# A narrower weight load and a changed order in the nine products of a scan step

## The chip, the cores and the metric

The kernel runs on one core of one Trainium2 chip. The metric is the device time of one launch in microseconds (us). Three runs of the kernel before are shown. A profile is one further execution, recorded by the hardware profiler.

## The reference

The input is a batch of 32 images of 48 channels, 64 rows and 128 columns in float32. Two layers follow each other. Each normalizes its input over groups of three channels, sends it through four scans and adds the result to its own input. Cut to what matters:

```python
def _conv1d(x, w, b):                       # 5 taps, 48 to 48 channels
    y = jax.lax.conv_general_dilated(x, w, window_strides=(1,), padding=[(2, 2)],
                                     dimension_numbers=('NCH', 'OIH', 'NCH'))
    return y + b[None, :, None]
def step(w, b):
    def f(carry, inp):
        nxt = inp + _conv1d(carry, w, b)
        return (nxt, nxt)
    return f
# rows downward (down_w), rows upward (down_w again), columns to the right (right_w),
# columns to the left (left_w): each is lax.scan(step(w, b), first, rest)
x = x + _L0_conv_ref(_gn(x), ...)
x = x + _L1_conv_ref(_gn(x), ...)
```

A step of a scan can't begin before the step ahead of it has ended: each takes the whole result of the last row (or column), convolves it along the row (or column) and adds the next input. There are 63 steps down, 63 up, 127 to the right and 127 to the left.

## The kernel before

**A step as nine products.** A row has 128 positions. Eight neighbouring positions and 48 channels make 384 pairs (position e from 0 to 7, channel), which are spread over three tiles of 128 partitions, called thirds here. The table `PIECES` says which position lies where: third 0 holds the positions 0 and 1 whole and 32 channels of position 2; third 1 holds 16 channels of position 2, then positions 3 and 4, and 16 channels of position 5 in its partitions 112 to 127; third 2 holds positions 6 and 7 and the rest of 5. Along the free dimension lie the 16 blocks of eight positions and 8 images, so 128 elements (for a column scan: 8 blocks of 8 and, again, the images and the halves of a pair of image groups, 128 elements too).

The convolution is then a product of a banded 384 x 384 matrix with the row. `PRODUCTS` lists its nine non-zero blocks as (input third i, output third o, shift s): seven within the block of eight and two across its border, (0, 2, 1) and (2, 0, -1), which read the neighbouring block. The border products have 96 weight columns (`BORDER`) and leave out the block at the edge, so that they stream 120 elements in a row step and 112 in a column step. All others have 128 weight columns (`FULL`) and stream 128. Five taps reach two positions far, so a part of a block can be zero: the weights are laid into zeroed tiles.

`step` walks through `PRODUCTS` in its order and issues one float32 matmul each (L706) into one of three PSUM tiles, one for each output third. The first product of an output third starts its accumulation, the last one ends it, and after it VectorE adds the bias and the input and writes the new row (L715). In the order of before, output third 0 is complete after five products, output third 2 after six and output third 1 after all nine. The next step begins with products of the input thirds 0 and 2; the first that needs third 1 is (1, 0, 0), its fifth. In the trace each float32 matmul stands as two weight loads (LDWEIGHTS) and two matmuls.

**The phases.** `PHASES` is an order of twelve phases written out by hand: eight row phases (down and up, for each of four groups of eight images in each of two layers) and four column phases (right and left, for each of two pairs of groups in each layer). Tiles are named after layer, group or pair and way: `step_01u` is layer 0, group 1, upward, `step_11l` layer 1, pair 1, to the left. A row phase has 126 steps, a column phase 254, and all together 2024.

**The work around the steps.** Everything else is put into the program between two steps by an agenda of due times, counted in steps: loading and storing rows and columns (SP's queue, some on ACT's and POOL's), scaling of the input by the normalization (ACT, L579), the additions of the residual (POOL, L638), permutations (POOL and ACT, L536 and L663), and the statistics, which use a few small matmuls of TensorE (L298 and L302). `in_order` keeps each engine in the order of the program. Each transfer or operation waits by semaphores for what it needs.

Of the kernel before, what the change touches and what calls it, by code (L numbers as in the profile page):

```python
# [33 lines left out]
C = 48  # L34
# [9 lines left out]
FULL = 128  # L44
# [22 lines left out]
    (2, 0, -1),  # L67
    (1, 0, 0),
    (1, 2, 0),
    (0, 1, 0),  # L70
    (1, 1, 0),
    (2, 1, 0),
)
BORDER = 2 * C


def weight_runs():
# [41 lines left out]
def kernel(  # L119
# [573 lines left out]
    def step(key, weights, b_at, src, inp, dst, whole, part):  # L693


        ps = [
            ps_step.tile([FULL, N], F32, tag=f"step{o}", name=f"step{o}_{key}")
            for o in range(NG)
        ]
        left = [sum(1 for p in PRODUCTS if p[1] == o) for o in range(NG)]  # L700
        seen = [0] * NG
        for i, o, s in PRODUCTS:
            seen[o] += 1
            m = BORDER if s else FULL
            at = FULL * (o - NG * s - i + 1)
            nc.tensor.matmul(  # L706
                part(whole(ps[o])[0:m], -s),
                weights[:, i, at : at + m],
                part(src(i), s),
                start=seen[o] == 1,  # L710
                stop=seen[o] == left[o],
            )
            if seen[o] == left[o]:
                layer, way = b_at
                nc.vector.scalar_tensor_tensor(  # L715
                    dst(o),
                    whole(ps[o]),
                    bd[:, o, layer, way : way + 1],
                    inp(o),
                    ALU.add,  # L720
                    ALU.add,
                )

    def row_step(k, h, prev, inp, name):
        _, layer, g = PHASES[k]

        def part(t, s):
            return t[:, max(0, s) * GB : N + min(0, s) * GB]

        step(  # L730
            f"{layer}{g}{name}{h}",
            wt[f"down{layer}"],
            (layer, DOWN),
            lambda i: prev[:, i],
            lambda o: inp[:, o],
            lambda o: row(k, h)[:, o],
            lambda ps: ps,
            part,
        )

    def col_step(k, way, v0, v1):
        _, layer, pair = PHASES[k]

        def col(v):
            kb, e = divmod(v, E8)
            j, kk = divmod(kb, KQ)
            view = slot[slots(k)[j % 3]].rearrange(
                "p (o m e k b) -> p o e k m b", o=NG, e=E8, k=KQ, b=GB
            )
            return lambda o: view[:, o, e, kk]  # L750

        def part(t, s):
            t = t.rearrange("p (s a) b -> p s a b", s=2)
            return t[:, :, max(0, s) : NH + min(0, s)] if s else t

        step(
            f"{layer}{pair}{'drl'[way]}{v1}",
            wt["right" if way == RIGHT else "left"],
            (layer, way),
            col(v0),  # L760
            col(v1),
            col(v1),
            lambda ps: ps.rearrange("p (m b) -> p m b", b=GB),
            part,
        )
# [422 lines left out]
```

## Time and profile before

| | |
|---|---|
| median of three runs | 4323.13 us (4319.51, 4324.4, 4323.13) |
| time of the profiled execution | 4327.19 us |
| its span, from the first to the last instruction | 4325.4 us |
| mean granted TensorE clock in the span | 0.979 |
| first matmul of a step, last matmul of a step (from the span's start) | 109 us, 4241 us |
| TensorE matmul busy | 4072.9 us (94%) |
| TensorE weight load busy | 4042.5 us (93%) |
| VectorE busy | 2177.4 us (50%) |
| ScalarE busy | 1337.2 us (31%) |
| GpSimd busy | 891.9 us (21%) |

Busy is the union of the durations of an engine's instructions. PE stands for TensorE's matmuls, PEld for its weight loads, which run beside the matmuls, DVE for VectorE, ACT for ScalarE, POOL for GpSimd and SP for SyncE, which issues transfers only. A line of a group names the source line, the engine, the operation, the tiles (out<-in), the active rows and weight columns of TensorE (128*96), partitions and elements streamed (128x112) and the count; then, behind the bar, busy time in us, the mean ns of one record, and behind the next bar the idle time just before these records with what ended most of it. A line of windows gives the stretch in us, its length, the busy time of the five engines, the granted clock, the share of the DMA engines' time and GB/s.

### The profile page before, as it was taken

How to read it: one execution, taken by the hardware profiler on the slowest of the kernel's cores; microseconds unless marked ns; L12 is line 12 of the kernel's file. 1: busy time of each engine (PE TensorE's matmuls, PEld its weight loads, DVE VectorE, ACT ScalarE, POOL GpSimd, SP SyncE). 2: the span in 40 equal slices, each digit the busy share in tenths (PEclk: the TensorE clock that was granted, in tenths of full speed). 3: DMA queues.
4: the chain of work that ended last, by engine and by line, in shares of the span. 5: the costliest groups of instructions: out<-in, count | busy, mean ns of one | idle time of the engine just before them, and what ended most of it. 6: DMA issues, size and time to landing. Idle time of an engine off the chain costs nothing. (4 is left out here: it accounts for less than half of the span.)

```text
span 4325.4 us, 89999 instructions
## 1 busy us (share of the span) xinstructions
PE 4072.9 (94%) x36624; PEld 4042.5 (93%) x36624; DVE 2177.4 (50%) x6554; ACT 1337.2 (31%) x2656; POOL 891.9 (21%) x859
## 2 busy tenths in 40 slices
PE   3898998998999999998999999999999999999992
PEld 1898998998999999998999999999999999999992
DVE  6344444446764445444446655444444444444443
ACT  1683301344794554300005773513000002110122
POOL 3472001234323010000004310000000024510352
PEclk9999999999999999999999999999999999999996
DMA  9999799966998989769507989929289049999999
GB/s 165 183 188 166 111 157 158 235 130 191 237 204 138 158 152 159 117 115 174 131 1 218 220 173 144 153 45 160 47 136 202 1 77 242 249 241 158 176 197 183
DMA packets 2117983, 680.35 MB, mean 157 GB/s; under 512 B 2006688, under 2 KB 2057408, under 8 KB 2077632
## 3 DMA queue, kind: packets, MB, share of 16 engines
q1 hardware_dynamic: 2019552, 582.30, 71.9%
q10 hardware_dynamic: 94816, 86.00, 9.7%
q0 software_dynamic: 3200, 6.30, 0.6%
q8 instruction: 288, 4.72, 0.5%
q14 instruction: 127, 1.04, 0.1%
HBM read 397.57 MB, written 295.99 MB: 160 GB/s over the span
## 5 line engine op out<-in xcount | busy, mean ns | idle before, releaser
L579 ACT ACTIVATE arena<-arena,offset,scale 128x256 f32<-128x256 f32 (+2 forms) x816 | 576.4, 800 | 423.9 <-PE step_12u L706 120.5
L638 POOL TENSOR_TENSOR arena<-arena 128x2048 f32<-128x2048 f32 x80 | 362.8, 4548 | 1469.2 <-PE step_10l L706 459.0
L536 POOL COPY arena<-arena 112x256 f32<-112x256 f32 x458 | 271.2, 651 | 561.5 <-DMA arena<-in_x 282.6
L706 PE MATMUL step_00r<-arena,early 128*128 128x128 f32 x2286 | 252.4, 274 | 15.3 <-DMA arena<-upa 14.2
L706 PEld LDWEIGHTS step_00r<-arena,early 128*128 128x128 f32 x2286 | 251.9, 187 | 15.8 <-issue 15.8
L706 PE MATMUL step_01r<-arena,early 128*128 128x128 f32 x2286 | 251.6, 274 | 14.0 <-DMA arena<-upa 14.0
L706 PEld LDWEIGHTS step_01r<-arena,early 128*128 128x128 f32 x2286 | 251.4, 187 | 14.2 <-issue 14.1
L706 PE MATMUL step_11r<-arena,early 128*128 128x128 f32 x2286 | 252.1, 274 | 8.6 <-DVE arena L715 8.6
L706 PEld LDWEIGHTS step_11r<-arena,early 128*128 128x128 f32 x2286 | 251.6, 187 | 9.0 <-DVE arena L715 8.9
L470 ACT ACTIVATE early<-arena 128x256 f32<-128x256 f32 x192 | 129.6, 675 | 412.2 <-DMA arena<-xin 319.9
L706 PE MATMUL step_00l<-arena,wleft 128*128 128x128 f32 x2286 | 252.2, 274 | 0.0
L706 PEld LDWEIGHTS step_00l<-arena,wleft 128*128 128x128 f32 x2286 | 251.8, 187 | 0.0
L706 PE MATMUL step_10l<-arena,wleft 128*128 128x128 f32 x2286 | 249.1, 272 | 0.0
L706 PE MATMUL step_11l<-arena,wleft 128*128 128x128 f32 x2286 | 249.1, 272 | 0.0
L706 PE MATMUL step_01l<-arena,wleft 128*128 128x128 f32 x2286 | 249.1, 272 | 0.0
L706 PE MATMUL step_10r<-arena,early 128*128 128x128 f32 x2286 | 249.1, 272 | 0.0
L706 PEld LDWEIGHTS step_10l<-arena,wleft 128*128 128x128 f32 x2286 | 249.0, 186 | 0.0
L706 PEld LDWEIGHTS step_11l<-arena,wleft 128*128 128x128 f32 x2286 | 249.0, 186 | 0.0
L706 PEld LDWEIGHTS step_01l<-arena,wleft 128*128 128x128 f32 x2286 | 249.0, 186 | 0.0
L706 PEld LDWEIGHTS step_10r<-arena,early 128*128 128x128 f32 x2286 | 249.0, 186 | 0.0
L663 ACT COPY arena<-arena 128x256 f32<-128x256 f32 x172 | 99.6, 656 | 404.2 <-POOL arena L638 152.9
L403 ACT ACTIVATE early<-arena 112x512 f32<-112x512 f32 x192 | 121.1, 631 | 305.6 <-DMA arena<-in_x 237.7
(176 smaller groups left out, 7070.1 us busy)
## 6 DMA issues: line engine op xcount, KB each, us to landing
arena<-in_x SPq DMA_DIRECT2D x48, 768.0 KB, 12.7
xin<-arena SPq DMA_DIRECT2D x96, 384.0 KB, 5.6
arena<-xin SPq DMA_DIRECT2D x96, 384.0 KB, 8.9
mid<-arena SPq DMA_DIRECT2D x96, 384.0 KB, 7.9
arena<-mid SPq DMA_DIRECT2D x192, 192.0 KB, 4.3
upb<-arena SPq DMA_DIRECT2D x192, 192.0 KB, 3.9
arena<-upb SPq DMA_DIRECT2D x96, 384.0 KB, 12.7
arena<-xin SPq DMA_DIRECT2D x186, 192.0 KB, 4.2
```

Source lines behind the costliest of these rows:

```text
L403: nc.scalar.activation(junk[0:P], piece, AF.Identity, accum_out=self.sum[:, at[0], at[1]],)
L470: nc.scalar.activation(junk[:, 0:n], view[:, b], AF.Identity, accum_out=self.sum[:, i, j : j + 1])
L536: copy(dst[:, r, q], src[:, r0 + r, q])
L579: nc.scalar.activation(args[0], args[0], AF.Identity, bias=args[2], scale=args[1])
L638: eng.tensor_tensor(unit, unit, nat, ALU.add)
L663: copy(by_w(perm)[:, a], src[:, a])
L706: nc.tensor.matmul(part(whole(ps[o])[0:m], -s), weights[:, i, at : at + m], part(src(i), s), start=seen[o] == 1, stop=seen[o] == left[o],)
```

## The change

The order of `PRODUCTS` changes in its last three entries: the product of input third 1 with output third 1 now comes before that of input third 0 with output third 1. The number of weight columns comes from a table, `COLUMNS`. The two border products keep their 96, and (0, 1, 0) has 128 - 48/3 = 112 instead of 128. It leaves out the partitions 112 to 127 of output third 1, which belong to position 5; the input third 0 holds positions 0 to 2, more than two away, so that these weights are zero. As (0, 1, 0) no longer writes all partitions, it can't be the product that starts the accumulation, which (1, 1, 0) does now. It streams 128 elements as before.

```diff
@@ -67,11 +67,12 @@
     (2, 0, -1),
     (1, 0, 0),
     (1, 2, 0),
+    (1, 1, 0),
     (0, 1, 0),
-    (1, 1, 0),
     (2, 1, 0),
 )
 BORDER = 2 * C
+COLUMNS = {(0, 2, 1): BORDER, (2, 0, -1): BORDER, (0, 1, 0): FULL - C // 3}
@@ -701,7 +702,7 @@
         for i, o, s in PRODUCTS:
             seen[o] += 1
-            m = BORDER if s else FULL
+            m = COLUMNS.get((i, o, s), FULL)
             at = FULL * (o - NG * s - i + 1)
```

## The prediction

> **What bounds the kernel now.** I read the page's engine table first, then TensorE's groups with the shapes kept apart, then the windows, and last the places where TensorE waits.
>
> ```profile
> span 4325.4 us, 89999 instructions
> PE 4072.9 (94%) x36624; PEld 4042.5 (93%) x36624; DVE 2177.4 (50%) x6554; ACT 1337.2 (31%) x2656; POOL 891.9 (21%) x859
> ```
>
> TensorE is the bound outside the head, the tail and some gaps; DVE has half its time free. The page's chain view helps with nothing here: it ends in one ScalarE copy of the last outputs.
>
> ```profile
> L715 DVE SCALAR_TENSOR_TENSOR arena<-step_10l,bd,arena 128x128 f32<-128x128 f32 x381 | 122.0, 348 | 126.9 <-PE step_10l L706 126.9
> L715 DVE SCALAR_TENSOR_TENSOR arena<-step_13u,bd,arena 128x128 f32<-128x128 f32 x186 | 59.5, 347 | 63.2 <-PE step_13u L706 63.0
> 3233.00:3482.00 249.00, 249.00 (x2289) 249.00 (x2288) 122.30 (x382) 0.00 (x0) 0.00 (x0) 1.00 0.46 97
> ```
>
> A step ends with three DVE additions, so busy plus idle over the steps is the step's period: (122.0 + 126.9)/127 = 1.960 us for a column step, (59.5 + 63.2)/62 = 1.979 for a row step. The window shows TensorE without a gap at full clock. There are 8 x 126 row and 4 x 254 column steps, 2024 in all.
>
> A step has 9 matmuls, each standing as two weight loads and two matmuls: 18 slots. What a slot costs comes out of the groups, because busy is a union: in a burst of k back-to-back records it is (k - 1) slots plus one record.
>
> ```profile
> L706 PE MATMUL step_10l<-arena,wleft 128*96 128x112 f32 x508 | 69.4, 259 | 0.0
> L706 PE MATMUL step_13u<-arena,early 128*96 128x120 f32 x252 | 36.1, 266 | 0.0
> L302 PEld LDWEIGHTS ps_r<-mean_c_r,maskp 112*128 112x128 f32 x24 | 3.0, 192 | 0.0
> L298 PEld LDWEIGHTS ps_r<-dev_r,mask_in 128*112 128x112 f32 x24 | 2.7, 178 | 0.0
> ```
>
> The border products (96 weight columns) come in fours, once per step. With 112 streamed columns: (69.4/127 - 0.259)/3 = 95.8 ns a slot; with 120: (36.1/63 - 0.266)/3 = 102.3 ns. The weights are the same, only the stream differs: these slots are **bound by the stream**, 0.82 ns a column, and 128 columns extrapolate to 109 ns. The two statistics rows stream only 8 columns, in bursts of six, so they show the **weight load**: 128 columns (3.0/4 - 0.192)/5 = 111.6 ns, 112 columns (2.7/4 - 0.178)/5 = 99.4, and 98.3 between the starts of single records (the rounding of 2.7 allows 97 to 102). So a slot is the longer of its weight load and the stream before it. A step adds up: 14 loads of 128 columns at 111.67 + one stream of 128 (into the first border product) 109.17 + 3 x 102.5 = 1980 ns; for columns 3 x 95.83 gives 1960. Both agree with the periods, which confirms 109.17.
>
> **What the Trainium skill says.** "TensorE: Matmul & The Clock Gate", section "LDWEIGHTS (loading the stationary operand)": a load takes its columns divided by 1.2, so 128 cost 106.7 and 112 cost 93.3 ns; the trace agrees on the difference (111.6 - 98.3 = 13.3) and adds 5 ns to each. The same page, "Back-to-back issue gap": N/2.4 + 2.5 ns for one pass. "FP8 and Floating Point Precision", "TensorE Precision Notes": true FP32 takes four passes. Two passes a record make 2 x 8/2.4 = 6.7 ns per 8 columns, as the border rows show. "Perfetto Trace Analysis", "Tensor Engine Instruction (MATMUL, LD_WEIGHTS)": a record starts with the prefetch and its end is estimated, so I use intervals, not durations.
>
> **The change part by part.**
>
> *The narrow load.* In each step the two loads of the third's product (0,1,0) shrink from 128 to 112 columns, 13.3 ns each. The stream beside them keeps 128 columns: the slot falls from 111.67 only to 109.17, by **2.5 ns**. 2 x 2.5 = 5.0 ns a step: 1.975 us for rows, 1.955 for columns. Times 2024: **10.1 us**. From both ends: 0, if the stream of 128 costs as much as its load; 13.3 ns a slot, 54 us, if loads could run ahead. I take 2.5, because in the border bursts loads of 96 columns keep strictly to the stream's 95.8 or 102.3 ns and gain nothing by being shorter.
>
> *The exchange.* (1,1,0) now opens the accumulation of output third 1 and (0,1,0) follows. Both inputs were waited for earlier in the step (third 0 at its first product, third 1 at (1,0,0)), and the DVE addition that frees third 1's accumulator is the one that (1,0,0) waits for. No wait, DMA or queue entry is added; SP, ACT and POOL keep their order. The last product is still (2,1,0), at the same place before the next step's four leading products, so the about 0.2 us between the end of DVE's third addition and the load that waits for it stays. Cost: 0; if that cover were gone, a DVE addition (0.35 us) would stand bare in each step.
>
> *The border products* take their 96 columns from a table instead of a condition: the same instructions, 0.
>
> *What swallows part of it.* The gain reaches the end only where the next gap follows TensorE's pace.
>
> ```profile
> L706 PE MATMUL step_00d<-arena,early 128*128 128x128 f32 x882 | 115.7, 283 | 23.7 <-DVE arena L715 16.9 <-DVE arena L590 6.8
> L706 PE MATMUL step_01d<-arena,early 128*128 128x128 f32 x882 | 112.3, 279 | 15.9 <-DVE arena L715 15.9
> L706 PE MATMUL step_02u<-arena,early 128*128 128x128 f32 x882 | 111.7, 278 | 9.3 <-DVE arena L715 9.3
> L706 PE MATMUL step_01r<-arena,early 128*128 128x128 f32 x1778 | 223.4, 278 | 14.0 <-DMA arena<-upa 14.0
> L706 PE MATMUL step_11r<-arena,early 128*128 128x128 f32 x1778 | 223.6, 277 | 8.6 <-DVE arena L715 8.6
> 4241.00:4326.00 85.00, 0.15 (x2) 0.00 (x0) 24.68 (x19) 18.89 (x33) 20.50 (x22) 0.51 1.28 174
> ```
>
> Each gap returns the gain made since the event that started the chain it waits for. The gaps of 00d and 01d (to 435 us) wait for input that arrives at its own pace; 141 steps lie before them: -0.7. The gap at 1363 (02u) hangs on input statistics whose chain TensorE last released at 1239: 62 steps, -0.3. The 14 us before 00r and 01r are a write and read back of the last rows, about 20 steps each: -0.2. Some 6 us in 11d around 2535 to 2572 follow a release at 2472: -0.3. The 8.6 us of 11r (at 3857) wait for loads behind a spill that starts with the step at 3794: 32 steps, -0.2. In the tail DMA is full (share 1.28), but its engines stood idle at 4053 to 4062 until TensorE released the results; only what is gained after that can vanish, 95 steps: -0.4. At half clock, some 11 steps: -0.1. Together -2.2.
>
> **Sum.** 10.1 - 2.2 = 7.9 us, 0.18%. The profiled execution took 4327.2 us around its span of 4325.4 and would come to 4319.3; the median of the runs shown is 4.1 us lower, 4323.1, and comes to **4315.2 us**. 0.2%, about what a measurement of this kernel can tell from no change, is 8.6 us: the forecast lies close under it.
>
> **The rivals.**
>
> *Nothing happens (chance 0.11).* The stream of 128 costs 111.67 itself, or the gaps swallow all. For it: recorded starts into the first border product lie 112 apart, although that load has 96 columns. Against it: then the step would be 2.5 ns longer than its period unless the way back into wide loads were shorter. Time: 4322 to 4324.
>
> *Loads run ahead (0.06).* Both loads give 13.3 ns: 26.7 a step, 54 us, 4269; half of it 4296. For it: the page above lets a weight load overlap earlier matmuls. Against it: the lockstep of the border bursts.
>
> *The switch back to wide loads costs (0.11), the slower end.* After a border burst the interval behind the first wide matmul is recorded as 118 ns in rows and 125 in columns, 6.5 and 13.3 over the usual. If that is a real restart cost, the change adds one more switch a step, at (2,1,0): 1008 x 6.5 + 1016 x 13.3 = 20 us, less 10 gained: +10, 4333. It decides from 5 ns a switch, where the gain is used up; from 9.3 the kernel is slower by over 0.2%. Against it: the interval ahead of it is short by as much (102.5 and 95.8), and 118.2 - 111.67 and 125 - 111.67 are just 109.17 less the two border streams: the start is recorded early, when the short stream ends, while the load is still running. With a 128-column stream this should vanish.
>
> **How the numbers follow.** My own case has 0.72. Its range is 4311 to 4319: from no loss in the gaps (10.1) and 2 us of run scatter below, to a loss of 4 and some scatter above; the runs shown differ by 4.9 us. Of it 0.30 gains over 8.6 us and 0.42 less. Faster by over 0.2%: 0.30 + 0.06 = 0.36. Within: 0.42 + 0.11 = 0.53. Slower: 0.11. The range of 8 in 10 takes in the case without effect and leaves out the far ends: 4310 to 4324.5.
>
> **What would show it.** In the profile after, the L715 groups give 1.975 and 1.955 us a step; the group 128*112 with 128 streamed columns appears in 4048 records; weight loads of 112 columns stand 109 ns apart. 1.98 and 1.96 would mean the stream costs what the load did, 1.953 and 1.933 that loads run ahead, over 1.98 a switch cost. If the periods are right and the time is not, the gaps at 1363, 2535, 3857 or the tail have grown by more than the 2.2 us above.

## The result and the profile after

| | before | after |
|---|---|---|
| median of 22 runs | 4324.85 us (4316.24 to 4334.18) | 4317.7 us (4301.99 to 4326.45) |
| profiled execution: time, span | 4327.19, 4325.4 us | 4318.23, 4316.5 us |
| ratio of the times | | 0.9982, interval 0.9974 to 0.9990 |

The changed kernel is faster by 0.18% (0.10 to 0.26%), 7.8 us by the ratio and 7.2 by the medians. The forecast was 7.9 us, 0.18%.

First the page of the changed kernel, then its groups. The line numbers of `step` are one higher than before.

```profile
span 4316.5 us, 89962 instructions
PE 4064.5 (94%) x36624; PEld 4034.0 (93%) x36624; DVE 2182.5 (51%) x6554; ACT 1337.3 (31%) x2656; POOL 891.0 (21%) x859
```

```profile
L716 DVE SCALAR_TENSOR_TENSOR arena<-step_10l,bd,arena 128x128 f32<-128x128 f32 x381 | 122.1, 348 | 126.2 <-PE step_10l L707 126.1
L716 DVE SCALAR_TENSOR_TENSOR arena<-step_13u,bd,arena 128x128 f32<-128x128 f32 x186 | 59.8, 349 | 62.7 <-PE step_13u L707 62.5
```

Busy plus idle over the steps gives the periods again: (122.1 + 126.2)/127 = 1.955 us in columns, (59.8 + 62.7)/62 = 1.976 in rows. Read from the starts of single records, averaged over the undisturbed steps, they are 1.9550 and 1.9750 us, against 1.9600 and 1.9800 before: 5.0 ns less in both, as forecast. TensorE, VectorE, ScalarE and GpSimd run as many instructions as before.

TensorE's groups, split by weight columns (the number after the star) and streamed elements:

```profile
L707 PE MATMUL step_10l<-arena,wleft 128*96 128x112 f32 x508 | 69.5, 259 | 0.0
L707 PE MATMUL step_10l<-arena,wleft 128*112 128x128 f32 x254 | 48.5, 273 | 0.0
L707 PE MATMUL step_13u<-arena,early 128*112 128x128 f32 x126 | 24.0, 273 | 0.0
```

The two matmuls of the narrow product make a burst of two, so a slot and one record: 48.5/127 - 0.273 = 0.109 us in columns and 24.0/63 - 0.273 = 0.108 in rows. That is the 109 ns of the stream, where a full load had taken 111.67. The border burst, (69.5/127 - 0.259)/3 = 96 ns, hasn't moved.

The gaps, in the groups with full weights:

```profile
L707 PE MATMUL step_00d<-arena,early 128*128 128x128 f32 x756 | 112.1, 285 | 23.3 <-DVE arena L716 16.4 <-DVE arena L591 6.8
L707 PE MATMUL step_01d<-arena,early 128*128 128x128 f32 x756 | 108.4, 279 | 18.2 <-DVE arena L716 17.7 <-ACT arena L580 0.5
L707 PE MATMUL step_02u<-arena,early 128*128 128x128 f32 x756 | 108.5, 279 | 9.9 <-DVE arena L716 9.9
L707 PE MATMUL step_01r<-arena,early 128*128 128x128 f32 x1524 | 215.9, 278 | 15.0 <-DMA arena<-upa 15.0
L707 PE MATMUL step_11r<-arena,early 128*128 128x128 f32 x1524 | 215.7, 278 | 6.7 <-DVE arena L716 6.7
```

The same gaps stand in the same places, some 2.3 us longer (01d), some 1.9 shorter (11r). One pair of executions can't settle which of them took back the gain: each gap differs by a microsecond or two from one execution to the next, and the spans of single executions spread as far as the whole effect. The head shows it too: the first step begins at 109.1 us before and at 104.7 after, with nothing changed ahead of it.

### The profile page after: what moved, and what is told of

Read it like the earlier page. It is cut to its first block, busy times and chain, and to the rows that moved or that the text cites. A ratio compares the mean times of both kernels' runs of the same rounds, so it can differ in the third digit from the quotient of the medians.

```text
span 4316.5 us, 89962 instructions
## 1 busy us (share of the span) xinstructions
PE 4064.5 (94%) x36624; PEld 4034.0 (93%) x36624; DVE 2182.5 (51%) x6554; ACT 1337.3 (31%) x2656; POOL 891.0 (21%) x859
```

## The experiments

For every run the step period in rows and columns was taken from the starts of single records, over the steps that no gap disturbs. These mostly repeat to 0.1 ns from phase to phase, so that one profiled execution tells 1 ns apart where times need many. The kernels with 96 and with 126 columns and the one with 64 columns and the full stream were executed once each, so only their periods are used.

### The exchange alone

```diff
-COLUMNS = {(0, 2, 1): BORDER, (2, 0, -1): BORDER, (0, 1, 0): FULL - C // 3}
+COLUMNS = {(0, 2, 1): BORDER, (2, 0, -1): BORDER}
```

> The exchange of the two products alone: (1,1,0) before (0,1,0), which keeps its 128 weight columns. My theory (the narrower load is the whole gain, the exchange costs and brings nothing): step periods of 1.980 us in rows and 1.960 in columns as before, and a time within 3 us of the kernel before. Rival (the order itself brings the gain, through a wait that comes later): periods of 1.975 and 1.955 us and some 7 us less. Rival (the order costs and the narrow load brings more than 5 ns a step): periods over 1.980 and 1.960.

Measured: periods of 1.9800 and 1.9600 us, ratio 0.9999 (0.9990 to 1.0007). Its groups:

```profile
L716 DVE SCALAR_TENSOR_TENSOR arena<-step_10l,bd,arena 128x128 f32<-128x128 f32 x381 | 122.1, 348 | 126.9 <-PE step_10l L707 126.8
L716 DVE SCALAR_TENSOR_TENSOR arena<-step_13u,bd,arena 128x128 f32<-128x128 f32 x186 | 59.6, 348 | 63.2 <-PE step_13u L707 63.0
```

The idle times are those of before, 126.9 and 63.2. The exchange is free, and the narrow load is the whole gain. One execution of this kernel had a span of 4316.2 us, as short as that of the changed kernel's profile: a warning against reading 9 us out of two single executions.

### How the gain depends on the columns

```diff
-COLUMNS = {(0, 2, 1): BORDER, (2, 0, -1): BORDER, (0, 1, 0): FULL - C // 3}
+COLUMNS = {(0, 2, 1): BORDER, (2, 0, -1): BORDER, (0, 1, 0): 96}
```

> (0,1,0) with 96 weight columns instead of 112, its stream of 128 elements kept; it leaves out 16 columns of weights that are not zero. Theory (the slot is the longer of its own weight load and the stream before it, and the stream of 128 takes 109.17 ns): nothing more is to be had, periods stay at 1.975 and 1.955 us. Rival (a shorter load still shortens the slot, since loads run ahead to some degree): 2 x 13.3 ns less, 1.948 and 1.928 us.

Measured: 1.9750 and 1.9550 us. Sixteen columns fewer than in the changed kernel bring nothing more.

```diff
-COLUMNS = {(0, 2, 1): BORDER, (2, 0, -1): BORDER, (0, 1, 0): FULL - C // 3}
+COLUMNS = {(0, 2, 1): BORDER, (2, 0, -1): BORDER, (0, 1, 0): 126}
```

> (0,1,0) with 126 weight columns, two fewer than before the change. Theory (longer of load and stream): a load of 126 takes 126/1.2 + 5 = 110.0 ns, 1.67 less than one of 128 and still over the stream's 109.17, so that a step loses 2 x 1.67 = 3.3 ns: 1.9766 us in rows and 1.9566 in columns. Rival (any load other than the full 128 columns takes another path and gives the whole 5.0 ns at once): 1.975 and 1.955. Rival (the gain is proportional to the columns left out): 5.0 x 2/16 = 0.6 ns, 1.9794 and 1.9594.

Measured: 1.9767 and 1.9567 us, 3.3 ns less than before; the recorded intervals of the narrow matmuls are 110.0 ns each. The groups of both, 96 columns first:

```profile
L716 DVE SCALAR_TENSOR_TENSOR arena<-step_10l,bd,arena 128x128 f32<-128x128 f32 x381 | 122.1, 348 | 126.2 <-PE step_10l L707 126.2
```

```profile
L716 DVE SCALAR_TENSOR_TENSOR arena<-step_10l,bd,arena 128x128 f32<-128x128 f32 x381 | 122.1, 348 | 126.4 <-PE step_10l L707 126.3
```

(122.1 + 126.2)/127 = 1.9551 and (122.1 + 126.4)/127 = 1.9567. With 126 columns the load still bounds the slot and the gain follows it; with 112 and with 96 the stream does. The loads measured, 111.67 ns for 128 columns, 110.0 for 126 and 98.3 for 112, all fit columns/1.2 + 5, which reaches 109.17 at 125 columns; 125 itself wasn't run. Loads that run further ahead are excluded, since then 96 columns would have brought more than 112.

### A shorter stream: which stream bounds a slot

```diff
+            into, rhs = part(whole(ps[o])[0:m], -s), part(src(i), s)
+            if (i, o, s) == (0, 1, 0):
+                into, rhs = (t[:, : 112 * t.shape[1] // N] for t in (into, rhs))
             nc.tensor.matmul(
-                part(whole(ps[o])[0:m], -s),
+                into,
                 weights[:, i, at : at + m],
-                part(src(i), s),
+                rhs,
```

> The changed kernel with (0,1,0) streaming 112 elements instead of 128, its 112 weight columns kept; it leaves out the contribution of this product to the last 16 elements. Theory (a slot is the longer of the load in it and the stream BEFORE it): only the slot between the two matmuls of (0,1,0) gets shorter, from 109.17 to the load's 98.33; the slot into the first one follows a stream of 128, the slot after the second one has a load of 128. A step takes 10.8 ns less than in the changed kernel: 1.9641 us in rows, 1.9441 in columns. Rival (the slot is that of the matmul's own stream and load): both fall, 21.7 ns less, 1.9533 and 1.9333. On the time: the steps give 15.8 ns x 2024 = 32 us against the kernel before. If the gaps keep the same share as I worked out (2.2 of 10.1, 411 of 2024 steps), 25 us remain; if the gaps keep a fixed amount whatever the gain, 29; if they keep much more, under 20.

Measured: 1.9642 and 1.9442 us, ratio 0.9943 (0.9930 to 0.9955). The first theory gave 1.9641 and 1.9441: a slot is set by the load in it and by the stream before it, and of three slots that a shorter stream could touch one fell. In the column phases the edit shortened the stream more than was meant. There `part` hands back the tile split into two halves, so that `t.shape[1]` is 2 and 112 * 2 // 128 is 1: one half is left, 64 elements, where the rows stream 112.

```profile
L710 PE MATMUL step_10l<-arena,wleft 128*112 128x64 f32 x254 | 40.4, 240 | 0.0
```

The forecast for the columns is the same with either, because the load of 98.33 ns is longer than a stream of 112 (95.83) and than one of 64 (109.17 less 64 times 0.83, which is 55.8).

This also settles what recorded starts are worth. Between the two matmuls of the product behind the narrow one the interval was recorded as 125.0 ns in rows and 165.0 in columns, 13.3 and 53.3 over the usual 111.67, which is what the streams of 112 and of 64 are short of 109.17. The periods came out exactly without any such cost, so these long intervals are displaced starts. In the changed kernel, where the narrow product streams 128, the interval is 111.9.

On the time, 15.8 ns x 2024 = 32.0 us of steps gave 24.6 us (19.4 to 30.2 by the interval), 77%. The proportional loss forecast 25; the fixed one, 29, lies inside the interval too.

### Sixty-four columns and elements

```diff
-COLUMNS = {(0, 2, 1): BORDER, (2, 0, -1): BORDER, (0, 1, 0): FULL - C // 3}
+COLUMNS = {(0, 2, 1): BORDER, (2, 0, -1): BORDER, (0, 1, 0): 64}
```

```diff
+                into, rhs = (t[:, : 64 * t.shape[1] // N] for t in (into, rhs))
```

> The changed kernel with (0,1,0) cut to 64 weight columns and 64 streamed elements; it leaves out most of this product. Theory of the slots: the first matmul's load still stands behind a stream of 128 (109.17), the second behind a stream of 64 (55.8) with a load of 64/1.2 + 5 = 58.3 ns, then a load of 128 (111.67): 55.8 ns a step less than before, 1.9241 us in rows and 1.9041 in columns, 113 us over 2024 steps. Theory of the losses (each gap returns what was gained since the event that started the chain it waits for, 411 of 2024 steps): 23 us vanish, of them 8 before 00d and 01d, 3.5 at 02u, 2 before the two column phases of layer 0, 2 each in 11d and 11r, 5 in the tail; the kernel gets faster by about 90 us. Rival (the gaps keep a fixed amount, some 3 us): 110 us. Rival (transfers become the bound where the steps get shorter): less than 75 us, with gaps in places that had none.

Measured: 2.2100 and 2.1900 us a step, 286 ns **more** than the 1.924 and 1.904 of the theory; ratio 1.0879 (1.0863 to 1.0896). The forecast was wrong. TensorE's groups of this kernel, weight loads first:

```profile
L710 PEld LDWEIGHTS step_10l<-arena,wleft 128*128 128x128 f32 x1524 | 189.7, 191 | 8.5
L710 PEld LDWEIGHTS step_10l<-arena,wleft 128*64 128x64 f32 x254 | 24.3, 134 | 15.4
L710 PE MATMUL step_10l<-arena,wleft 128*64 128x64 f32 x254 | 41.7, 246 | 0.0
```

The last number of a load's line is idle time ahead of it, which was 0.0 in this phase before: 15.4 us over 127 steps is 0.12 us ahead of the narrow loads, 8.5 us is 0.07 ahead of the wide ones behind them. There the loads pause while matmuls still run. In the single records the first narrow load and the first wide one after it start 1 to 2 ns before their own matmuls (the second narrow one 53), where loads in the rest of the step start 94 to 110 ns before.

The Trainium skill offers a cause: "TensorEngine Tiling (Array Packing)", section "Key Properties", says that a change of the tiling mode drains TensorE, and its section "When to Use Tiling" puts column tiling at 64 columns or fewer. Two runs part the columns from the elements.

```diff
-COLUMNS = {(0, 2, 1): BORDER, (2, 0, -1): BORDER, (0, 1, 0): FULL - C // 3}
+COLUMNS = {(0, 2, 1): BORDER, (2, 0, -1): BORDER, (0, 1, 0): 64}
```

> (0,1,0) with 64 weight columns and its full stream of 128; it leaves out the weights of 64 columns. The run with 64 columns and 64 elements took 2.210 us a step instead of 1.924. Theory now ([...]its loads are no longer hidden): the same serial pattern, and since the streams are 53.3 ns longer each, about 2.26 to 2.32 us in rows. Rival (the short stream of 64 elements was the cause): 1.975 in rows and 1.955 in columns, as with 96 columns.

Measured: 2.3142 and 2.2942 us, 339 ns over the 1.975 and 1.955 that 64 columns would take if they behaved as 96 do. It takes 104 ns more than with 64 elements.

The second has the stream cut to 64 elements, by the same line as above, and 65 columns:

```diff
-COLUMNS = {(0, 2, 1): BORDER, (2, 0, -1): BORDER, (0, 1, 0): FULL - C // 3}
+COLUMNS = {(0, 2, 1): BORDER, (2, 0, -1): BORDER, (0, 1, 0): 65}
```

> (0,1,0) with 65 weight columns and 64 streamed elements; it leaves out most of this product. Theory (drain only at 64 columns or fewer; above that a slot is the longer of its load and the stream before it): 65/1.2 + 5 = 59.2 ns in the slot between the two matmuls, so 2.5 + 52.5 = 55.0 ns a step less than before: 1.925 us in rows and 1.905 in columns, 111 us over 2024 steps. Rival (the short stream is the cause): over 2.1 us. On the time: about a fifth vanished or was hidden in the runs so far (32 us of steps gave 24.6, 466 gave 380, 120 gave 93), so 111 give 89 (82 to 95) if the share holds; less than 75 if transfers become the bound; 105 and more if the loss is a fixed amount.

Measured: 1.9250 and 1.9050 us, as forecast. One column more takes the step from 2.2100 to 1.9250 us. Their groups, 64 columns with 128 elements, then 65 columns with 64:

```profile
L716 DVE SCALAR_TENSOR_TENSOR arena<-step_10l,bd,arena 128x128 f32<-128x128 f32 x381 | 122.1, 348 | 169.2 <-PE step_10l L707 169.2
```

```profile
L719 DVE SCALAR_TENSOR_TENSOR arena<-step_10l,bd,arena 128x128 f32<-128x128 f32 x381 | 122.1, 348 | 119.9 <-PE step_10l L710 119.9
```

(122.1 + 169.2)/127 = 2.294 and (122.1 + 119.9)/127 = 1.906. The columns decide, not the stream. The runs agree with the page on the place, between 64 and 65. That an ordinary product of 64 columns changes the tiling mode is not said there and no trace shows it: the mechanism stays open, and fewer than 64 columns were not run.

The time of this run missed its forecast: 111 us of steps gave 72.5 us (66.5 to 78.1, ratio 0.9832), 65% instead of 80. Its profiled execution, 9 us longer than the run's median, shows where gaps grew:

```profile
L710 PE MATMUL step_02d<-arena,early 128*128 128x128 f32 x756 | 112.1, 288 | 9.6 <-issue 7.0 <-DVE arena L719 2.6
L710 PE MATMUL step_11d<-arena,early 128*128 128x128 f32 x756 | 110.2, 285 | 7.3 <-issue 7.3
L710 PE MATMUL step_00u<-arena,early 128*128 128x128 f32 x756 | 108.6, 283 | 5.9 <-DVE arena L719 5.7
L710 PE MATMUL step_10u<-arena,early 128*128 128x128 f32 x756 | 108.5, 283 | 4.8 <-DVE arena L719 4.8
```

From the first matmul of one phase to that of the next, phase 02d took 139.6 us against 129.0 before, although its 63 steps should have given 3.5: 14 lost. Phase 10u lost 7 and the tail, 92.8 against 84.6 us, 8. Nothing was foreseen in 02d or 10u. In 02d VectorE's additions wait for ScalarE's scaling of rows (waits from 1215 to 1275 us; each line gives the total, the number and the longest of the waits in us):

```profile
DVE arena L719 <- ACT arena L580: 12.6, 4, 6.6
ACT arena L580 <- DMA arena<-xin: 5.3, 2, 3.2
```

TensorE's 7.0 us of "issue", time for which the profile shows no releaser, belong to these: its longest gap ends 0.1 us after the addition that had waited 6.6 us. The 7.3 us in 11d are for the most part one gap that ends in the same way, 0.1 us after an addition that had waited 6.7 us for ScalarE. And in 10u a statistics operation of VectorE, placed by steps, waits for sums that ScalarE makes at its own pace, and holds up the additions queued behind it (waits from 1605 to 1630):

```profile
PEld step_10u L710 <- DVE arena L719: 5.1, 2, 4.4
DVE neg_x_x L425 <- ACT early L396: 5.1, 1, 5.1
```

That these two would come back in further executions of this kernel wasn't tried.

### Taking away a part of the cover

```diff
     (0, 0, 0),
     (2, 2, 0),
-    (0, 2, 1),
     (2, 0, -1),
     (1, 0, 0),
+    (0, 2, 1),
     (1, 2, 0),
```

> The changed kernel in the order (0,0,0), (2,2,0), (2,0,-1), (1,0,0), (0,2,1), (1,2,0), (1,1,0), (0,1,0), (2,1,0): the first product that reads third 1 stands one product earlier, the rest keeps its cover; all is computed. By the slots alone, with the border products in two bursts of two, a step takes 1.9817 us in rows and 1.9683 in columns. Theory (the exchange in the change was free because its products stay behind and ahead of the same waits; VectorE's third addition ends some 665 ns after the start of the last matmul, and a load follows about 60 ns later): the load of (1,0,0) would be due 660 ns after that start and waits 65 ns (30 to 100): about 2.047 and 2.036 us a step, 3.5% slower. Rival (the cover was larger than I read it, the order is of no matter): 1.982 and 1.968 and a time within 15 us of before. Rival (a wait costs the whole addition of 350 ns): over 2.25.

Measured: 2.0333 us in rows and 2.0251 in columns (2.0266 in the two scans to the right of layer 0), ratio 1.0216 (1.0199 to 1.0233). Over the slots' 1.9817 and 1.9683 the wait is 52 ns in rows and 57 in columns, near the 65 forecast. TensorE's groups of this kernel:

```profile
L707 PE MATMUL step_10l<-arena,wleft 128*128 128x128 f32 x1524 | 243.2, 282 | 0.0
L707 PE MATMUL step_10l<-arena,wleft 128*96 128x112 f32 x508 | 90.1, 259 | 0.0
L707 PE MATMUL step_10l<-arena,wleft 128*112 128x128 f32 x254 | 48.5, 273 | 0.0
```

The narrow product still has its 109 ns slot (48.5). The border products, now in two bursts of two, lie 90.1/254 - 0.259 = 96 ns apart as ever. The wait shows between them and (1,0,0): its first load is recorded 158 ns behind the load ahead of it in rows, and its matmul 170 ns before the next. That it waits for VectorE can be read from the single records too: the load starts 53 ns after the end of the third addition in rows and columns alike, where before it started 203 ns after it in rows and 183 in columns. So the first product that reads third 1 has no place to give away: one product earlier costs more than ten times what the narrow load brings. By its steps the kernel should be 120 us slower, (53.3 x 1008 + 65.1 x 1016) ns; it was 93, 2.2% and not the 3.5% expected: that figure counted the steps alone, with a wait some 10 ns too long, and its own periods make 3.4%.

### What of a step's change reaches the time

| run | steps give | time | share |
|---|---|---|---|
| changed kernel | -10.1 us | -7.8 (-4.3 to -11.2) | 77% (43 to 111) |
| stream of 112 (columns: 64) | -32.0 | -24.6 (-19.4 to -30.2) | 77% (61 to 94) |
| 65 columns, 64 elements | -111.3 | -72.5 (-66.5 to -78.1) | 65% (60 to 70) |
| one product earlier | +120.0 | +93 (86 to 101) | 78% (72 to 84) |
| 64 columns and elements | +465.5 | +380 (373 to 387) | 82% (80 to 83) |

Times are the ratio less one, times the median of before in the same comparison. Part of the change vanishes in both directions: what a gap swallows of a gain it gives back when steps get longer. The two small changes can't tell how much, and of the three large ones the one with 65% lies clear of the other two, so this is no fixed share.

The gaps of the run with 64 columns and elements, whose steps are 230 ns longer, show where it happens (one profiled execution):

```profile
L710 PE MATMUL step_01d<-arena,early 128*128 128x128 f32 x756 | 112.0, 284 | 0.0
L710 PE MATMUL step_02u<-arena,early 128*128 128x128 f32 x756 | 113.0, 285 | 0.0
L710 PE MATMUL step_01r<-arena,early 128*128 128x128 f32 x1524 | 228.6, 286 | 14.1 <-DMA arena<-upa 14.1
L710 PE MATMUL step_11r<-arena,early 128*128 128x128 f32 x1524 | 226.7, 285 | 1.0 <-DVE arena L719 1.0
```

Before they were 15.9, 9.3, 14.0 and 8.6 us. The gaps of 01d and 02u close, 11r's all but closes, those of 11d close too, and the tail was 57.4 us long instead of 84.6. The gap ahead of 01r stays as it was. A gap that has closed gives back nothing more. The run with 64 columns and 128 elements has the same pattern (0.0, 0.0, 13.3 and 0.0 us).

## Why the prediction was right

**The slots.** The reading that a slot is the longer of its load and the stream before it gave 5.0 ns a step; measured 5.0. The extrapolated 109.17 ns for a stream of 128 was the number that all hung on; it stands in the narrow burst of the profile after, and the runs with 126, 112 and 96 columns enclose it.

**The bounds of this step** are settled: that the stream takes as long as the load is excluded by the periods, and loads that run ahead by the periods and by the run with 96 columns.

**The exchange** was costed at nothing, with the place of the waits as the reason; alone it measured nothing, and the run that moved a product of third 1 showed the cover to be real. The price that I named for the loss of the whole cover, a bare addition of 0.35 us, was not put to the test: the run took away one of the four products ahead of third 1, and that cost 0.05 us.

**The rival of the switch back to wide loads** fell: no long interval behind the narrow product, and with a shortened stream long recorded intervals without any cost.

**What the gaps swallow.** 2.2 us were forecast as the sum of six places; 10.1 less 7.8 is 2.3, with an interval from below 0 to 5.8. The size agrees, but the changed kernel alone couldn't have shown it, and the larger changes show only that such a loss exists: 65 to 82% were passed on. One slip in the sum is small: in the tail 95 steps of 5.0 ns make 0.5 and not 0.4 us. Of the places, the run with 64 columns and elements bears out most. With steps 230 ns longer the input phases to the end of 01d gave back 30 us, where the list's 141 steps make 32, the tail 27 for 95 steps' 22, 11r 10 for 32 steps' 7, and the gaps of 02u and 11d closed. The gaps ahead of 00r and 01r should have given back 4.6 us each for their 20 steps and hardly moved (15.3 to 13.8 and 14.0 to 14.1), so this term, 0.2 us of the 2.2, doesn't hold. In the other direction, with 65 columns and gains eleven times those of the change, the input phases (8 us to the end of 01d) and 11d (4) lost what the list gave them, 7.7 and 3.3; 02u lost 1 instead of 3.3, while 02d, 10u and some of the tail lost what the list didn't have.

**The runs' scatter** was taken as 2 us; the 22 runs of after spread over 24. The gain is good to some 3.5 us, and the forecast's closeness to it, 7.9 against 7.8, is partly luck. So is the place of the median in its range: the kernel before had a median of 4324.9 us beside it, but of 4317.6 to 4318.9 in the three later comparisons, which is nearly as far apart as the change is worth. Only medians of one comparison can be set against each other.

## What to carry to other kernels

In a stream of load and matmul pairs, work out both bounds from bursts of different widths and streams before shortening one: a load cut from 128 to 112 columns was worth 2.5 ns and not 13.3, because the stream beside it came next. Keep a narrowed load above 64 columns when its neighbours are wide. And don't count a step's gain in full: gaps that wait for something other than the steps pass on only a part (here 65 to 82% in the three large changes). A deliberate large change to the step measures that part far better than a small one. It should go the way that is asked about, since a gap that has closed gives back nothing more.

## What the runs showed of the hardware that had not been expected

A float32 product of 64 weight columns between products of 128 cost 286 ns more a step (with 64 elements) and 339 more (with 128) than the same product would cost by its slots, while 65 columns cost nothing: 2.2100 against 1.9250 us. TensorE's loads pause ahead of the first narrow load, which is recorded 312 to 313 ns behind the wide load ahead of it, against 111.7 elsewhere, and again ahead of the first wide load after the product. Doubling the stream adds 104 ns, about the 107 that two matmuls with 64 columns more each take at 53.3 ns.
